# Two-layer graph attention on one core: the shared slot tile is gathered last, and three loads become one transfer each

## The chip, the cores and the metric

The kernel runs on one core of a Trainium2 chip. The metric is the device time of one execution in microseconds (us). The engines are named as the profile names them: PE (matrix products), DVE and ACT (elementwise work), POOL (here it issues the gathers) and SP (here it issues plain transfers). Each engine works through its own instructions in a fixed order and waits on semaphores.

## The reference

A pre-normalised graph network over 3125 nodes with 768 features and 50000 drawn edges plus one self loop per node, sorted by destination (the layer adds a second self loop for every node):

```python
h = jnp.maximum(_layernorm(x, axis=-1), 0.0)
# layer 1: 4 heads x 256, layer 2: 1 head x 768
def gat_conv(x, edge_index, W, a_src, a_dst, bias, heads, out_ch, concat):
    xl = (x @ W).reshape(n, heads, out_ch)
    e = leaky_relu(alpha_src[src] + alpha_dst[dst], 0.2)
    e = exp(e - segment_max(e, dst)[dst])
    alpha = e / (segment_sum(e, dst)[dst] + 1e-16)
    return segment_sum(xl[src] * alpha, dst) + bias
h1 = relu(layer_norm(gat_conv(h, ..., W1, ...), g1, be1)) + (h @ Wr1 + br1)
h2 = layer_norm(gat_conv(h1, ..., W2, ...), g2, be2) + (h1 @ Wr2 + br2)
out = x + h2
```

## The kernel before

Everything is float32. The change touches layer 2 alone. Its nodes are cut into 25 **node tiles** `b` of 128 (the last has 53). The edges of a node tile, sorted by destination, stand in 17 **slot tiles** `j` of 128 slots (`J = 17`; the last node tile has 8). Node tiles hang together in chains of three (`CHAIN = 3`): where `shared(b)` holds, that is for `b` with `b % 3` of 1 or 2, the last slot tile (16) of node tile `b - 1` and the first (0) of `b` are one and the same tile of 128 slots, gathered once. A chain so needs 17 + 16 + 16 = 49 gathers.

For every slot tile POOL issues one indirect transfer (`gather`, lines 206 to 217) that fetches 128 rows of 784 values from the table of layer 2 into one of 36 buffers `g0` to `g35` (`RING = 36`), used in turn. `slots_due` (line 1333) lists the gathers in their planned order, and `fetch` (line 1338) issues them: node tile by node tile, and in a node tile by the five rounds of `ROUNDS = [(0, 5, 9, 13), (1, 6, 10, 14), (4, 11, 15), (2, 8, 16), (3, 7, 12)]`. A gather is issued once the buffer 36 places earlier in the plan is free. Tile 16 stands at the end of round 3, and three tiles of round 4 come behind it. Where it is shared, its buffer is free only after round 0 of the next node tile. The planned order is what the code writes; the order on POOL's own queue is made by a scheduler, which may put a later gather ahead of one whose buffer it expects to come free later. The order on PE, ACT and DVE is written out by hand (`manual_schedule`, line 1465).

The loop over node tiles (line 1482) has the five rounds too. In round `k` of node tile `b`:

- PE adds up the weighted rows of the round's slot tiles (`summed`, line 1421, in a PSUM tile `pa`), which frees their buffers and lets `fetch` go on.
- ACT copies the logits of the gathered rows of node tile `b + 1` into `slots` (`values`, line 1360), at `k` of 0, 1 and 2 for rounds 2, 3 and 4 of that node tile. Rounds 0 and 1 were copied at the end of the node tile before.
- At `k = 2`, once all slot tiles of `b + 1` have landed and are copied, PE transposes them (`mix`, line 1378), and the softmax of `b + 1` follows on DVE and ACT. PE's rounds 3 and 4 of `b` stand behind that transposition in PE's order.
- PE also works at the residual product `pr` (line 1314, recorded as L190) of node tile `b + 3`, eight steps per node tile: one each in rounds 1 and 2, four and then two in round 4.

So PE can't finish node tile `b` before the last gather of node tile `b + 1` has landed.

SP loads, per node tile, `h1` (the residual's input, 512 KB, `load_h1`, in four transfers of two of its eight slices, asked for at residual steps 0 to 3), `xr` (the rows of x, 384 KB, `load_xr`, in two halves, at steps 3 and 4), `own` (the node tile's own rows of the table, 384 KB, `load_own`, in two halves, in rounds 0 and 1) and `hot` (80 KB). In the built program SP's and ACT's transfers use eight semaphores in turn, and POOL's eight others: a transfer waits for the landing of the earlier one that had its semaphore. So at most eight gathers are on their way at once, and SP gets held up where eight of its transfers are.

Of the kernel before, what the change touches and what calls it, by code (L numbers as in the profile page):

```python
# [69 lines left out]
def in_order(  # L70
# [59 lines left out]
    def tiles_of(b):  # L130
        return J if b < NB - 1 else JL
# [1100 lines left out]
    with tc.tile_pool(name="m2", bufs=1, reuse_waits="tile") as mp, \  # L1232
# [35 lines left out]
        for k in range(NK2):  # L1268
            nc.gpsimd.dma_start(wr2[:, k, :], Wr2[k * 128:(k + 1) * 128, :])

        def load_h1(b, q=nc.sync, ks=slice(0, NK2)):
            if b < NB:
                if b not in h1s:
                    h1s[b] = small([128, NK2, P], "h1", bufs=3)
                r = rows_of(b)
                q.dma_start(h1s[b][:, ks, :r], h1T_d[b][:, ks, :r])

        def load_xr(b, cs=slice(0, C2)):
            if b < NB:
                xr = xrs[b] = xrs.get(b) or small([128, C2], "xr", bufs=5)  # L1280
                load_rows(nc.sync, xr[:, cs], x[:, cs], b)

        load_h1(0, nc.gpsimd)
        load_h1(1, nc.gpsimd)
# [17 lines left out]
        def residuals():  # L1302

            for b in range(NB):
                h1, xr = h1s.pop(b), xrs[b]
                r = rows_of(b)
                pm = pp.tile([P, 2, 512], F32, name="pr")
                for k in range(NK2):
                    if k < NK2 // 2:
                        load_h1(b + 2, ks=slice(2 * k, 2 * k + 2))  # L1310
                    if k in (3, 4):
                        load_xr(b + 1, slice((k - 3) * f, (k - 2) * f))
                    for i in range(2):
                        dense(pm[:, i, :f], h1[:, k, :], wr2[:, k, i * f:(i + 1) * f], r,
                              start=(k == 0), stop=(k == NK2 - 1), at=half_at(b, i).start)
                    if k == NK2 - 1 and r == P:
                        nc.vector.tensor_add(pm[:, :, :f], pm[:, :, :f], halves(ball_b))
                        nc.vector.tensor_add(halves(xr), pm[:, :, :f], halves(xr))
                    elif k == NK2 - 1:
                        nc.vector.tensor_add(xr[:r], xr[:r], ball_b[:r])  # L1320
                        for i in range(2):
                            cs = slice(i * f, (i + 1) * f)
                            nc.vector.tensor_add(xr[:r, cs], pm[half_at(b, i), i, :f], xr[:r, cs])
                    yield
# [3 lines left out]
        def filled(n):  # L1328
            for _ in range(n):
                next(fill, None)  # L1330

        gs = {}
        slots_due = [(b, j) for b in range(NB) for k in ROUNDS for j in k
                     if j < tiles_of(b) and not (j == 0 and shared(b))]
        order_of = {s: i for i, s in enumerate(slots_due)}
        asked, unused = 0, set(range(len(slots_due)))

# [9 lines left out]
                    gs[b + 1, 0] = g  # L1347
                asked += 1

        def load_own(b, cs=slice(0, C2)):  # L1350
            if b < NB:
                if b == NB - 1 and b not in owns:
                    owns[b] = small([128, NK2, P], "h1", bufs=3).rearrange("p k n -> p (k n)")[:, :C2]
                own = owns[b] = owns.get(b) or small([128, C2], "own")
                load_rows(nc.sync, own[:, cs], table2[:, cs], b)

        def values(b, k):
            for j in ROUNDS[k]:
# [106 lines left out]
        with tc.manual_schedule(engines={PE, ACT, DVE}):  # L1465
# [16 lines left out]
            for b in range(NB):  # L1482
                pa = pp.tile([P, 2, 512], F32, name="pa", bufs=2)
                opened = set()
                last = b + 1 == NB - 1
                for k in range(len(ROUNDS)):
                    if last and k == 0:
                        load_own(b + 1)
                        for i in range(2, len(ROUNDS)):
                            values(b + 1, i)  # L1490
                        made = softmax(b + 1)
                        next(made)
                    summed(b, k, pa, opened)
                    if k < 2:
                        next(ending, None)
                        if 0 < b < NB - 1:
                            load_own(b, slice(k * f, (k + 1) * f))
                    if b + 1 < NB and not last:
                        if k < 3:
                            values(b + 1, k + 2)  # L1500
                        if k == 2:
                            made = softmax(b + 1)
                            next(made)
                    if k == 2:
                        for _ in ending:
                            pass
                    if k == 4:
                        ending = finish(b, pa)
                        next(ending)
                    if k == 4:  # L1510
                        filled(STEPS[k])
                    if b + 1 < NB and k == (1 if last else 4):
                        next(made)
                        next(made, None)
                        totals2(b + 1)
                        if last:
                            own_share(b + 1)
                    filled(REST if k == 4 else STEPS[k])
                if b + 2 < NB:
                    values(b + 2, 0)  # L1520
                    values(b + 2, 1)
# [474 lines left out]
```

## Time and profile before

| | |
|---|---|
| time, median of 3 runs | 1760.58 us (1757.6 to 1760.94) |
| the profiled execution | 1760.3 us, of which the span from the first to the last instruction is 1758.5 us |
| PE busy | 1632.8 us (93% of the span) |
| DVE, ACT, POOL busy | 1005.1, 457.3, 872.0 us |
| layer 2: first gather issued, last gather issued, end | 1187.73, 1725.4, 1758.5 us |
| gathers of layer 2 | 400, of 401 KB each where all 128 rows are fetched |
| moved by DMA between 1240 and 1690 us | 168.48 MB, 374 GB/s |

A row of a timeline or of a chain begins with the start in us from the span's start and the duration in us; then come engine, line, operation and tiles. In square brackets stands how long the engine was idle before it and what ended that. Gathers are named here by node tile and slot tile, (6,12) for instance, by counting POOL's gathers from the first of the layer and taking their tiles from the built order.

### The profile page before, as it was taken

How to read it: one execution, taken by the hardware profiler on the slowest of the kernel's cores; microseconds unless marked ns; L12 is line 12 of the kernel's file. 1: busy time of each engine (PE TensorE's matmuls, PEld its weight loads, DVE VectorE, ACT ScalarE, POOL GpSimd, SP SyncE). 2: the span in 40 equal slices, each digit the busy share in tenths (PEclk: the TensorE clock that was granted, in tenths of full speed). 3: DMA queues.
4: the chain of work that ended last, by engine and by line, in shares of the span. 5: the costliest groups of instructions: out<-in, count | busy, mean ns of one | idle time of the engine just before them, and what ended most of it. 6: DMA issues, size and time to landing. Idle time of an engine off the chain costs nothing.

```text
span 1758.5 us, 31362 instructions
## 1 busy us (share of the span) xinstructions
PE 1632.8 (93%) x11522; PEld 936.7 (53%) x11522; DVE 1005.1 (57%) x2604; ACT 457.3 (26%) x1312; POOL 872.0 (50%) x908
## 2 busy tenths in 40 slices
PE   7999999999989999999999999997988988988984
PEld 5666666566656556556556555544444443443431
DVE  7784343788864566556565566641444544544545
ACT  2222342000122112212122122122333433433432
POOL 2000012100055766667666667627767667667662
PEclk9999999899989999999999999998999999989987
DMA  7833546533189999999999999969999999999994
GB/s 241 280 120 110 147 129 208 233 132 129 37 313 369 409 400 404 393 403 409 404 393 406 375 374 387 399 228 373 373 370 395 370 359 396 371 357 392 364 328 156
DMA packets 188644, 546.69 MB, mean 311 GB/s; under 512 B 32120, under 2 KB 80632, under 8 KB 188354
## 3 DMA queue, kind: packets, MB, share of 16 engines
q0 software_dynamic: 99632, 386.94, 57.9%
q1 hardware_dynamic: 84456, 147.27, 23.9%
q10 hardware_dynamic: 4394, 10.39, 1.5%
q8 instruction: 94, 1.54, 0.4%
q14 instruction: 68, 0.56, 0.1%
HBM read 492.19 MB, written 65.62 MB: 317 GB/s over the span
## 4 chain that ended last, share of the span: by engine, by line
PE 76%; DMA 14%; DVE 5%; issue 2%; ACT 2%; POOL 1%; SPq 0%; POOLq 0%; DVEq 0%; ACTq 0%
PE pr L190 18%; PE p L190 13%; PE pm L190 12%; PE pa L775 11%; PE pm L1027 7%; PE pa L1421 6%; DMA g<-table,idx_s 5%; DMA g<-table,hi_s 4%; PE pq L580 3%; PE mix L1378 1%; DMA w<-in_L_gnn_W_dram 1%; PE p L1190 1%; DMA h<-h1T_d 1%; DMA s<-slo_d 1%; PE pt L859 1%
## 5 line engine op out<-in xcount | busy, mean ns | idle before, releaser
L210 POOL DMA_INDIRECT g<-table,idx_s x393 | 378.8, 964 | 358.4 <-PE pq L610 170.9
L214 POOL DMA_INDIRECT g<-table,hi_s x423 | 433.6, 1025 | 203.8 <-issue 85.3
L190 PE MATMUL pr<-wr,h 128*128 128x384 f32 x768 | 277.3, 507 | 2.9 <-issue 2.1
L190 PE MATMUL p<-w,h1T 128*128 128x384 f32 (+1 forms) x768 | 267.7, 496 | 0.0
L775 PE MATMUL pa<-g,w 128*32 128x256 f32 x3912 | 246.7, 386 | 8.3 <-DVE w L752 5.6
L190 PEld LDWEIGHTS pr<-wr,h 128*128 128x128 f32 x768 | 143.7, 197 | 112.8 <-issue 35.9
L190 PEld LDWEIGHTS p<-w,h1T 128*128 128x128 f32 x768 | 139.8, 189 | 113.0 <-issue 21.4
L775 PEld LDWEIGHTS pa<-g,w 128*32 128x32 f32 x3912 | 119.7, 110 | 128.3 <-issue 23.8
L1421 PE MATMUL pa<-g,w 128*32 128x384 f32 x1956 | 176.7, 499 | 2.6 <-DVE v L1455 2.6
L752 DVE TENSOR_TENSOR w<-oh,al 128x128 f32<-128x128 f32 (+1 forms) x416 | 132.3, 318 | 51.9 <-PE pa L775 27.2
L190 PE MATMUL pr<-h0k,wr 128*128 128x256 f32 (+1 forms) x576 | 143.0, 395 | 2.5 <-DMA h0k<-h0T_d 2.5
L1027 PE MATMUL pm<-h0g,wr 128*128 128x512 f32 x288 | 133.1, 609 | 0.0
L190 PE MATMUL pm<-w,h0g 128*128 128x344 f32 x432 | 131.5, 459 | 0.3 <-ACT h0g L861 0.3
L190 PE MATMUL pm<-w,h0l 128*128 128x344 f32 x432 | 129.5, 454 | 0.0
L190 PEld LDWEIGHTS pr<-h0k,wr 128*128 128x128 f32 x576 | 106.9, 192 | 32.7 <-issue 10.7
L958 POOL DMA_DIRECT2D hot_d<-ohd x25 | 13.4, 535 | 213.2 <-DVE own L531 123.6
L1421 PEld LDWEIGHTS pa<-g,w 128*32 128x32 f32 x1956 | 57.5, 111 | 113.1 <-issue 104.7
L751 DVE TENSOR_SCALAR oh<-iota_f,rel_s 128x32 f32<-128x32 f32 (+1 forms) x416 | 114.4, 275 | 3.7 <-issue 3.5
L190 PEld LDWEIGHTS pm<-w,h0g 128*128 128x128 f32 x432 | 81.6, 193 | 40.1 <-issue 1.4
L190 PEld LDWEIGHTS pm<-w,h0l 128*128 128x128 f32 x432 | 80.5, 190 | 39.1 <-issue 0.2
L1382 DVE CUSTOM_DVE_ANT_0 mix<-mix,pen 128x640 f32<-128x640 f32 x25 | 20.8, 832 | 129.7 <-PE mix L1378 129.7
L1223 DVE COPY asad<-p 128x2 f32<-128x2 f32 (+1 forms) x25 | 4.0, 159 | 155.3 <-ACT row L1221 155.3
(295 smaller groups left out, 1751.4 us busy)
## 6 DMA issues: line engine op xcount, KB each, us to landing
s<-slo_d SPq DMA_DIRECT2D x25, 544.0 KB
table<-row SPq DMA_DIRECT2D x24, 512.0 KB
own<-table SPq DMA_DIRECT2D x24, 512.0 KB
h1T_d<-h1T SPq DMA_DIRECT2D x24, 512.0 KB
h<-h1T_d SPq DMA_DIRECT2D x88, 128.0 KB
table<-row SPq DMA_DIRECT2D x24, 392.0 KB
ring<-in_x_dram SPq DMA_DIRECT2D x24, 384.0 KB
out_dram<-z ACTq DMA_DIRECT2D x24, 384.0 KB
```

The source lines that it names most:

```text
L190: nc.tensor.matmul(out_, lhsT, rhs, start=start, stop=stop)
L210: nc.gpsimd.indirect_dma_start(out=g, out_offset=None, in_=table[:, :], in_offset=bass.IndirectOffsetOnAxis(ap=idx_s[:, c], axis=0))
L214: nc.gpsimd.indirect_dma_start(out=g, out_offset=None, in_=table[:, :], in_offset=bass.IndirectOffsetOnAxis(ap=idx_k[:, c], axis=0), bound ...
L580: nc.tensor.matmul(q[:, j], oh[:P, o:o + 128], tabs[:, i], start=(i == 0), stop=(i == 2))
L751: nc.vector.tensor_scalar(oh, iota_f[:, lo:hi], rel_s[:, c:c + 1], None, op0=OP.is_equal)
L752: nc.vector.tensor_tensor(w, oh[:, None, :].to_broadcast([128, heads, hi - lo]), al[:, POS[j], :, b:b + 1].to_broadcast([128, heads, hi - ...
L775: nc.tensor.matmul(pa[p0:p0 + 32, o // f, o % f:o % f + n], w[:, o // cols, :], g[:, o:o + n], start=to not in opened, stop=False, skip_gr ...
L859: nc.tensor.transpose(pt[:, k, :r], xt[:, (k0 + k) * 128:(k0 + k + 1) * 128], ident[:r, :r])
L1027: nc.tensor.matmul(pm, wr1[:, k, m * 128:(m + 1) * 128], groups[gi][:, k, :], start=(k == 0), stop=(k == NK1 - 1))
L1190: nc.tensor.transpose(pt[:, k, :r], z[:, (k0 + k) * 128:(k0 + k + 1) * 128], ident[:r, :r])
L1382: nc.vector.tensor_tensor_reduce(out=sums_, in0=sums_, in1=pen, scale=1.0, scalar=-BIG, op0=OP.add, op1=OP.max, accum_out=top)
L1421: nc.tensor.matmul(pa[p0:p0 + 32, i, :f], w_, g[:, i * f:(i + 1) * f], start=(i, q) not in opened, stop=False, skip_group_check=True)
```

## The change

The gathers of a node tile that shares its last slot tile with the next one are reordered in the plan: slot tile 16 comes after 3, 7 and 12 in place of before them (`due`). When its values are copied and when it is summed is as before. Besides, `h1`, `xr` and `own` are loaded by one transfer each: `h1` at residual step 1, `xr` at step 3, `own` in round 0. The bytes are the same.

```diff
-        def load_h1(b, q=nc.sync, ks=slice(0, NK2)):
+        def load_h1(b, q=nc.sync):
             if b < NB:
-                if b not in h1s:
-                    h1s[b] = small([128, NK2, P], "h1", bufs=3)
+                h1s[b] = small([128, NK2, P], "h1", bufs=3)
                 r = rows_of(b)
-                q.dma_start(h1s[b][:, ks, :r], h1T_d[b][:, ks, :r])
-
-        def load_xr(b, cs=slice(0, C2)):
+                q.dma_start(h1s[b][:, :, :r], h1T_d[b][:, :, :r])
+
+        def load_xr(b):
             if b < NB:
                 xr = xrs[b] = xrs.get(b) or small([128, C2], "xr", bufs=5)
-                load_rows(nc.sync, xr[:, cs], x[:, cs], b)
+                load_rows(nc.sync, xr, x, b)
...
                 for k in range(NK2):
-                    if k < NK2 // 2:
-                        load_h1(b + 2, ks=slice(2 * k, 2 * k + 2))
-                    if k in (3, 4):
-                        load_xr(b + 1, slice((k - 3) * f, (k - 2) * f))
+                    if k == 1:
+                        load_h1(b + 2)
+                    if k == 3:
+                        load_xr(b + 1)
...
-        slots_due = [(b, j) for b in range(NB) for k in ROUNDS for j in k
-                     if j < tiles_of(b) and not (j == 0 and shared(b))]
+
+        def due(b):
+
+            js = [j for k in ROUNDS for j in k if j < tiles_of(b) and not (j == 0 and shared(b))]
+            return sorted(js, key=lambda j: j == J - 1) if shared(b + 1) else js
+
+        slots_due = [(b, j) for b in range(NB) for j in due(b)]
...
-        def load_own(b, cs=slice(0, C2)):
+        def load_own(b):
             if b < NB:
                 if b == NB - 1 and b not in owns:
                     owns[b] = small([128, NK2, P], "h1", bufs=3).rearrange("p k n -> p (k n)")[:, :C2]
                 own = owns[b] = owns.get(b) or small([128, C2], "own")
-                load_rows(nc.sync, own[:, cs], table2[:, cs], b)
+                load_rows(nc.sync, own, table2[:, :C2], b)
...
                     if k < 2:
                         next(ending, None)
-                        if 0 < b < NB - 1:
-                            load_own(b, slice(k * f, (k + 1) * f))
+                        if k == 0 and 0 < b < NB - 1:
+                            load_own(b)
```

The first place where it shows is **POOL's queue at the end of node tile 3's gathers**. `g29_12765` is buffer 29 for the gather (3,12) before; the rows above it are (3,2), (3,8), then the shared tile (3,16) in `g26_12660`, (3,3) and (3,7), and behind them (4,5), (4,9) and (4,13) in `g30` to `g32`. Before:

```order
L210 DMA g25_12658<-table2_65,idx_s_98 128x784
L214 DMA g26_12660<-table2_65,hi_s_99 128x784
L210 DMA g27_12704<-table2_65,idx_s_98 128x784
L210 DMA g28_12706<-table2_65,idx_s_98 128x784
L210 DMA g30_12767<-table2_65,idx_s_98 128x784
L210 DMA g31_12769<-table2_65,idx_s_98 128x784
L210 DMA g32_12771<-table2_65,idx_s_98 128x784
L210 DMA g29_12765<-table2_65,idx_s_98 128x784
L210 DMA g33_12773<-table2_65,idx_s_98 128x784
```

And now:

```order
L210 DMA g25_12639<-table2_65,idx_s_98 128x784
L210 DMA g26_12641<-table2_65,idx_s_98 128x784
L210 DMA g27_12684<-table2_65,idx_s_98 128x784
L210 DMA g28_12686<-table2_65,idx_s_98 128x784
L214 DMA g29_12696<-table2_65,hi_s_99 128x784
L210 DMA g30_12700<-table2_65,idx_s_98 128x784
L210 DMA g31_12702<-table2_65,idx_s_98 128x784
L210 DMA g32_12750<-table2_65,idx_s_98 128x784
L210 DMA g33_12752<-table2_65,idx_s_98 128x784
```

Before, the scheduler had put three gathers of node tile 4 ahead of node tile 3's last one, whose buffer 29 held the shared tile (1,16); now node tile 3's five last gathers stand together and the shared tile (3,16) is the last of them. The same swap of three places is there for (6,12), (9,12) and so on to (21,12), seven times in all; the first gathers of these node tiles (3,0) and so on also stood behind three others, and now don't.

The second place is **ACT's copies of node tile 3's logits** for rounds 3 and 4. Before:

```order
L1360 ACTIVATE slots1_12190<-g25_12658 128x32
L1360 ACTIVATE slots1_12190<-g26_12660 128x32
L1360 ACTIVATE slots1_12190<-g27_12704 128x32
L1360 ACTIVATE slots1_12190<-g28_12706 128x32
L1360 ACTIVATE slots1_12190<-g29_12765 128x32
```

And now:

```order
L1364 ACTIVATE slots1_12190<-g25_12639 128x32
L1364 ACTIVATE slots1_12190<-g29_12696 128x32
L1364 ACTIVATE slots1_12190<-g26_12641 128x32
L1364 ACTIVATE slots1_12190<-g27_12684 128x32
L1364 ACTIVATE slots1_12190<-g28_12686 128x32
```

ACT's order of slot tiles is the same ((3,8), (3,16), (3,3), (3,7), (3,12)), so the copy of the gather that is issued last now stands ahead of three others.

The third place is **SP's queue at the start of layer 2**. `own` is node tile 0's, the `xr` are node tiles 1 to 4, and the `h` are the residual's inputs from node tile 2 on. Before:

```order
L227 DMA own<-table_65 128x768
L227 DMA xr<-in_x_dram 128x384 x4
L1258 DMA hot<-hot_d 128x640
L227 DMA xr<-in_x_dram 128x384 x2
L1276 DMA h_12306<-h1T_d 128x256 x4
L227 DMA xr<-in_x_dram 128x384 x2
L1276 DMA h_12333<-h1T_d 128x256 x4
L1276 DMA h_12397<-h1T_d 128x256 x4
L1258 DMA hot<-hot_d 128x640
```

And now:

```order
L227 DMA own<-table_65 128x768
L227 DMA xr<-in_x_dram 128x768 x2
L1258 DMA hot<-hot_d 128x640
L227 DMA xr<-in_x_dram 128x768
L1275 DMA h_12308<-h1T_d 128x1024
L227 DMA xr<-in_x_dram 128x768
L1275 DMA h_12331<-h1T_d 128x1024
L1275 DMA h_12391<-h1T_d 128x1024
L1258 DMA hot<-hot_d 128x640
```

The loads keep their places among each other, here and in every later node tile, where SP's sequence is `h1`, `xr`, `own`, `hot` before and now. There are nine transfers to a node tile before and four now, so the eight semaphores go round less often. PE's, ACT's and DVE's instructions keep their order.

## The prediction

> **What bounds the kernel now.** The first view is PE's list of waits over the whole run (what waited for what: us in total, times, longest):
>
> ```profile
> PE mix L1378 <- ACT slots L1360: 72.7, 14, 9.7
> PE pt L859 <- DVE ring L839: 8.7, 2, 7.5
> ```
>
> PE is 93% busy; of what it waits, nearly all is one place in layer 2, the transposition of the copied logits. The second view is PE's timeline there:
>
> ```profile
> 1285.61 1.33 PE L1378 MATMUL mix<-ident,slots 128*128 128x128 f32 x5 [7.13 <-ACT slots L1360]
> ...
> 1300.21 2.79 PE L1421 MATMUL pa<-g,w 128*32 128x384 f32 x32
> ...
> 1305.85 0.77 PE L1378 MATMUL mix<-ident,slots 128*128 128x128 f32 x5
> ...
> 1350.51 1.33 PE L1378 MATMUL mix<-ident,slots 128*128 128x128 f32 x5 [6.95 <-ACT slots L1360]
> ...
> 1365.09 2.79 PE L1421 MATMUL pa<-g,w 128*32 128x384 f32 x32
> ...
> 1523.25 0.77 PE L1378 MATMUL mix<-ident,slots 128*128 128x128 f32 x5 [0.96 <-ACT slots L1360]
> ...
> 1681.89 1.33 PE L1378 MATMUL mix<-ident,slots 128*128 128x128 f32 x5 [7.56 <-ACT slots L1360]
> ```
>
> A long wait comes once per chain of three node tiles, seven times from 1285.61 (for node tile 3) to 1681.89 (for 21); in between PE waits about 1 us or not at all (1305.85, 1523.25). What ends it is on ACT's timeline, which is the third view, for the wait at 1350.51:
>
> ```profile
> 1336.29 1.16 ACT L1360 ACTIVATE slots<-g 128x32 f32<-128x32 f32 x9
> ...
> 1345.44 0.23 ACT L1360 ACTIVATE slots<-g 128x32 f32<-128x32 f32 x1 [0.81 <-DMA g<-table,idx_s]
> 1350.23 0.23 ACT L1360 ACTIVATE slots<-g 128x32 f32<-128x32 f32 x1 [4.56 <-DMA g<-table,idx_s]
> ```
>
> The last copies are those of (6,7) and (6,12). Gathers before them landed about 1.2 us apart, but between these two there are 4.8 us. The fourth view, POOL's timeline, says why:
>
> ```profile
> 1302.44 0.94 POOL L210 DMA_INDIRECT g<-table,idx_s  x1 [3.71 <-PE pa L1421]
> ...
> 1337.70 0.95 POOL L210 DMA_INDIRECT g<-table,idx_s  x1 [0.30 <-ACT slots L1360]
> 1338.95 0.96 POOL L210 DMA_INDIRECT g<-table,idx_s  x1 [0.30 <-issue]
> 1340.22 0.95 POOL L210 DMA_INDIRECT g<-table,idx_s  x1 [0.30 <-issue]
> 1341.47 0.95 POOL L210 DMA_INDIRECT g<-table,idx_s  x1 [0.30 <-issue]
> 1342.72 0.95 POOL L210 DMA_INDIRECT g<-table,idx_s  x1 [0.30 <-ACT slots L1360]
> ...
> 1362.83 0.96 POOL L210 DMA_INDIRECT g<-table,idx_s  x1 [0.30 <-issue]
> 1367.32 0.94 POOL L210 DMA_INDIRECT g<-table,idx_s  x1 [3.53 <-PE pa L1421]
> ...
> 1700.18 0.94 POOL L210 DMA_INDIRECT g<-table,idx_s  x1 [3.94 <-PE pa L1421]
> ```
>
> (6,7) is issued at 1337.70, then (7,5), (7,9), (7,13), and (6,12) only at 1342.72. POOL issues one gather per 1.254 us (0.95 and a gap of 0.30) whatever happens, except where the ring is full: at 1302.44, 1367.32 and so on it had been idle until PE's round 0 of node tiles 3, 6, ... freed a buffer.
>
> So layer 2 runs in a **loop** of one chain: round 0 of node tile 3 (PE 1300.21) lets POOL go on (1302.44); 32 gathers later (6,12) is issued (40.28 us); it is copied 7.51 us after that; PE goes on 0.28 later (1350.51); PE's rest of node tile 5 and round 0 of node tile 6 take 16.81 up to POOL's next release (1367.32). The sum is 64.88 us; over six loops, from 1302.44 to 1700.18, the mean is 66.29. Two floors lie below it. PE alone needs less (it waits). POOL alone, at 49 gathers of 1.254, needs 61.4. The DMA engines are the third thing near its limit:
>
> ```profile
> 600.00:800.00 200.00, 199.70 (x1665) 117.20 (x1664) 120.13 (x402) 40.49 (x114) 135.10 (x133) 1.00 1.02 401
> 1240.00:1690.00 450.00, 397.53 (x2495) 192.26 (x2488) 208.14 (x386) 178.60 (x546) 320.48 (x336) 0.94 1.01 374
> 1260.00:1300.00 40.00, 32.87 (x191) 16.76 (x189) 16.51 (x32) 15.35 (x46) 29.58 (x31) 0.91 1.02 389
> 1320.00:1360.00 40.00, 33.05 (x218) 15.88 (x211) 18.62 (x34) 14.97 (x42) 30.47 (x32) 0.91 1.03 394
> ```
>
> The last column of these stretches is GB/s: 374 on average in layer 2, 389 and 394 where POOL doesn't pause, 401 in layer 1. The third from last is PE's granted clock.
>
> **The order of the gathers.** The built order puts (6,16) where (7,5) was, at 1338.95 in place of 1342.72: three gathers earlier, 3.77 us. Its buffer was freed in round 4 of node tile 4, some 20 us before, so it waits for nothing. The landing moves with it. Against that, ACT copies (6,16) ahead of (6,3), (6,7) and (6,12), which have landed: three copies more behind the awaited one, 1.16 us / 9 = 0.13 each, 0.39 together. PE goes on 3.77 - 0.39 = 3.38 us earlier, at each of the seven waits.
>
> Where does it go? PE's round 0 releases POOL 3.38 earlier; POOL was idle there 3.5 to 3.9, of which 0.30 is its usual gap, so it takes up all of it. The loop becomes 66.29 - 3.38 = 62.91, still 1.5 above POOL's floor. After the last loop nothing is moved: node tile 23 doesn't share its last slot tile with 24. Sum: 7 x 3.38 = **23.7 us**. Late next is the same landing: PE still waits some 3.6 to 4.2 us there (6.95 to 7.56 less 3.38). The gathers for the other two node tiles of a chain have little slack (0.96 at 1523.25), and PE now comes 3.4 us earlier for them: waits of a microsecond or so will appear there, but they cost nothing as long as the long one behind them ends with a landing that POOL's count sets.
>
> After a wait of 6.95 the transposition takes 1.33, after one of 0.96 it takes 0.77, so PE's clock has sunk in the long ones (0.91 in both stretches that hold one, 1.00 in layer 1). Whether 3.6 to 4.2 us still sinks it lies between a wait of 2.65 (quoted below at 1235.13, matmuls as fast as ever) and those of 7. I take it as sunk, so nothing is gained there; if not, PE's 16.81 shrink by 1.4 or so (0.56 of the transposition, the rest in the matmuls behind it), and POOL's floor decides. The Trainium skill (TensorE: Matmul & The Clock Gate, Part 1) has the clock halve after an idle window of about 3.4 us. The rows agree with that from both sides; by it most of these waits would still be cold, which gives my sum, and the first rival's if the waits come out a little shorter.
>
> **The merged loads.** The same bytes in larger pieces; the queues between 1240 and 1690 us (packets, MB, share of 16 engines' time):
>
> ```profile
> q0 software_dynamic: 26922, 133.18, 77.9%
> q1 hardware_dynamic: 26286, 27.37, 18.6%
> q10 hardware_dynamic: 2736, 7.47, 4.2%
> ...
> h<-h1T_d SPq DMA_DIRECT2D x74, 128.0 KB
> own<-table SPq DMA_DIRECT2D x40, 192.0 KB
> xr<-in_x_dram SPq DMA_DIRECT2D x38, 192.0 KB
> ```
>
> q1 holds SP's loads: 27.37 MB in 18.6% of 16 x 450 us, 20.4 GB/s per engine; the results on q10, whose rows are whole, get 24.7, the gathers 23.7. At q10's rate q1's bytes take 231 us of engine time less, 14 us of all 16 engines in 450, or 3% of the DMA time. This lies beside the loop, not on it, and I count 0. It is cover: a loop of 62.91 needs 374 x 66.29 / 62.91 = 394 GB/s, which is what the stretch at 394 moves. Unmerged loads would leave no room, merged ones some 3%. Bounds: at best the landing of 7.51 gets shorter by 0.2 (3% of it), 1.5 us over the seven; at worst the rival below. SP's own issuing is no term: SP waits for data and semaphores, nobody for SP.
>
> **The start of layer 2.** Here the merge changes when loads go out. Two pieces of the chain of waits, then SP's and PE's timelines:
>
> ```profile
> 1188.94 11.96 DMA own<-table
> 1200.92 18.07 DMA h<-h1T_d
> ```
>
> ```profile
> 1193.63 0.33 SPq L1258 DMA_DIRECT2D hot<-hot_d  x1
> ```
>
> ```profile
> 1210.22 2.46 SPq L227 DMA_DIRECT2D xr<-in_x_dram  x2
> 1214.67 17.37 SPq L1276 DMA_DIRECT2D h<-h1T_d  x8
> ```
>
> ```profile
> 1216.96 1.33 PE L1378 MATMUL mix<-ident,slots 128*128 128x128 f32 x5 [9.72 <-ACT slots L1360]
> 1219.12 7.65 PE L190 MATMUL pr<-wr,h 128*128 128x384 f32 x16 [0.83 <-DMA h<-h1T_d]
> ...
> 1235.13 2.79 PE L1421 MATMUL pa<-g,w 128*32 128x384 f32 x32 [2.65 <-DVE v L1455]
> ```
>
> `h1` of node tile 2 waits until `own` has landed (1200.92), as its semaphore comes round; with half the transfers it has the semaphore that `hot` got at 1193.63 before. So it lands before PE wants it, and PE's 0.83 go. But `xr` of node tile 4 and `h1` of 3 and 4 (0.39 + 0.52 + 0.52 = 1.43 MB) can go out too before node tile 0's last gather, which PE waits for at 1216.96. If all of it lands ahead, that is 1.43 MB / 394 GB/s = 3.6 us. Bounds -0.8 and +3.6; I take +1.0, since the last of it waits for PE's second residual block, and all of it shares the engines with the gathers. All that follows moves along.
>
> **Sum** against the profiled run's own 1760.3 (span 1758.5 and 1.8 around it; the median of the runs is 1760.58, 0.3 above): 1760.3 - 23.7 + 1.0 = **1737.6 us**, and about 1738 as a median.
>
> **The rivals.**
>
> *POOL's floor.* If PE's clock holds, the loop falls to 61.4: 1760.3 + 1.0 - 3.4 - 6 x 4.9 = 1728.5. For it: the waits come out near the 2.65 that did no harm. Against it: every loop would have to run without a single pause of POOL's.
>
> *The landing gets longer.* With POOL hardly pausing the DMA engines never drain, and each landing takes 1 to 2 us more: 1738 + 7 x (1 to 2) = 1745 to 1752. For it: 394 needed where 389 to 394 is what was moved in such stretches. Against it: larger pieces.
>
> *The other waits count.* Waits for the other two node tiles of a chain add up with the long one, up to 1.2 each: the gain falls to 1 us a loop, 1754. Against it: the long wait has 3 us to swallow them.
>
> *Slower: the merged loads stand ahead of the awaited gather.* `h1`, `xr` and `own` of a node tile, 1.31 MB, no longer trickle in small pieces between gathers but go in front of them: 1.31 / 394 GB/s = 3.3 us on a landing of 7.5, and the order's gain is spent. Past 10.0 us (eight gathers of 1.254 on their way) POOL itself is held up, as perhaps already once at the start:
>
> ```profile
> 1226.92 0.95 POOL L210 DMA_INDIRECT g<-table,idx_s  x1 [1.66 <-issue]
> ```
>
> A landing of 10.8 would hold it 0.8 us at each load of the chain (three node tiles), 7 x 2.4 = 17 us: 1777. Where only the awaited landing is hit, 1761. Against it: SP issued these pieces back to back before, too (eight in 17.37 us only where semaphores lacked). The Trainium skill (DMA: Bandwidth & Descriptors, Queues, rings and completion order) has each DMA engine go round its queues a packet at a time. By that rule larger packets do give SP's queue a larger share against the gathers; no row here shows it yet.
>
> That the change doesn't do what it says is answered by the built order: the three places are gone.
>
> **How the numbers follow.** Forecast 0.57 (own range 1731 to 1744); POOL's floor 0.14; longer landings 0.13; the other waits 0.08; slower 0.08. 0.2% (3.5 us) is about what a measurement of this kernel tells from no change. Faster: 0.57 + 0.14 + 0.13 and half of the other waits, 0.88; the same: the other half and a quarter of the last case, 0.06; slower: 0.06. The range, 1728 to 1752, takes in the floor, the start's bounds and the longer landings.
>
> **What would show it.** Right: the last copy of node tile 6 is (6,12) with its gather long landed, and the awaited one, (6,16), starts some 1.2 us behind (6,7)'s place; the seven waits at `mix` fall to 3 to 4 us; POOL's idle before its releases all but goes; layer 2 moves about 394 GB/s. Wrong: landings from issue to copy well over 8 us, POOL idle on `issue` over 0.3 in midstream, long waits for the other two node tiles, or round 0 of node tile 0 later than 1239.

## The result, and the profile after

| | before | after |
|---|---|---|
| median, same chip | 1758.0 us (5 runs, 1757.6 to 1760.94) | 1746.25 us (5 runs, 1738.72 to 1747.39) |
| ratio, 95% interval | | 0.9916 [0.9893, 0.9940] |
| profiled execution | 1760.3 us, span 1758.5 | 1742.3 us, span 1740.5 |
| DMA packets, of them under 2 KB | 188644, 80632 | 172393, 55625 |

The change gains 0.84% (0.6 to 1.07%): 11.75 us between the medians, 18.0 between the two profiled executions. The executions of the changed kernel scatter more (8.7 us against 3.3), and the profiled one is among its shorter ones. What follows is read from it.

PE's list of waits (us in total, times, longest):

```profile
PE mix L1382 <- ACT slots L1364: 53.4, 16, 11.9
```

19.3 us less than before, though the count went from 14 to 16 and the longest, at the start of the layer, from 9.7 to 11.9. PE's timeline shows which became shorter and which are new:

```profile
1285.04 0.98 PE L1382 MATMUL mix<-ident,slots 128*128 128x128 f32 x5 [3.58 <-ACT slots L1364]
...
1347.19 1.33 PE L1382 MATMUL mix<-ident,slots 128*128 128x128 f32 x5 [3.62 <-ACT slots L1364]
...
1388.20 0.77 PE L1382 MATMUL mix<-ident,slots 128*128 128x128 f32 x5 [1.78 <-ACT slots L1364]
1411.15 0.80 PE L1382 MATMUL mix<-ident,slots 128*128 128x128 f32 x5 [4.06 <-ACT slots L1364]
...
1559.14 1.33 PE L1382 MATMUL mix<-ident,slots 128*128 128x128 f32 x5 [2.71 <-ACT slots L1364]
...
1602.09 0.77 PE L1382 MATMUL mix<-ident,slots 128*128 128x128 f32 x5 [3.87 <-ACT slots L1364]
...
1665.89 1.33 PE L1382 MATMUL mix<-ident,slots 128*128 128x128 f32 x5 [5.49 <-ACT slots L1364]
```

The waits once per chain fell from about 7 us to between 3.6 and 5.5, at node tile 15 even to 0.24, with 2.71 at the next one (1559.14); for the other two node tiles of a chain waits of 1 to 3 us came up (1388.20 as well; the one there was 1.31 before). Their cause is again on ACT's and POOL's timelines, here for node tile 9:

```profile
1402.41 0.23 ACT L1364 ACTIVATE slots<-g 128x32 f32<-128x32 f32 x1 [1.32 <-DMA g<-table,idx_s]
...
1405.94 0.33 ACT L1364 ACTIVATE slots<-g 128x32 f32<-128x32 f32 x2
1410.52 0.58 ACT L1364 ACTIVATE slots<-g 128x32 f32<-128x32 f32 x4 [4.25 <-DMA g<-table,hi_s]
```

```profile
1302.09 0.95 POOL L210 DMA_INDIRECT g<-table,idx_s  x1 [1.76 <-PE pa L1425]
...
1338.49 1.01 POOL L214 DMA_INDIRECT g<-table,hi_s  x1 [0.30 <-issue]
...
1364.12 0.95 POOL L210 DMA_INDIRECT g<-table,idx_s  x1 [0.67 <-PE pa L1425]
...
1401.71 1.01 POOL L214 DMA_INDIRECT g<-table,hi_s  x1 [0.30 <-issue]
...
1683.82 0.95 POOL L210 DMA_INDIRECT g<-table,idx_s  x1 [2.63 <-PE pa L1425]
```

The gather waited for is now the shared tile's (`hi_s`). (9,16) is issued at 1401.71, its copy starts at 1410.52, 8.81 us later, three others behind it in the same x4; PE goes on at 1411.15. POOL's idle before its releases went from 3.5 to 4.0 us to between 0.3 and 2.9. The loop, release to release, is (1683.82 - 1302.09) / 6 = 63.62 us, from 66.29. The landing of a gather is here the time from its issue to the start of its copy on ACT. Averaged over the six loops, in us:

| part of the loop | before | after | difference | predicted |
|---|---|---|---|---|
| release to the issue of the awaited gather | 40.55 | 36.82 | -3.73 | -3.77 |
| issue to the start of its copy (landing) | 7.90 | 8.72 | +0.82 | 0 |
| start of the copy to PE | 0.28 | 0.63 | +0.35 | +0.39 |
| PE to the next release | 17.56 | 17.45 | -0.11 | 0 |
| loop | 66.29 | 63.62 | -2.67 | -3.38 |

Six loops give -16.0. The first release is 0.35 earlier (1302.44 to 1302.09), and from the last release to the end it is 56.6 in place of 58.3 us: together -18.0, the whole difference of the spans. Two stretches by engine (the last three columns are PE's granted clock, DMA share and GB/s):

```profile
1240.00:1690.00 450.00, 416.67 (x2631) 200.02 (x2627) 216.04 (x401) 181.06 (x568) 330.64 (x347) 0.96 1.01 384
...
1320.00:1360.00 40.00, 36.09 (x227) 17.85 (x220) 18.95 (x34) 14.47 (x41) 30.25 (x32) 0.96 1.01 394
```

Layer 2 now moves 384 GB/s, 374 before. At the start of the layer, SP's queue and then PE's:

```profile
1193.04 0.33 SPq L1275 DMA_DIRECT2D h<-h1T_d  x1
...
1197.88 11.07 SPq L1275 DMA_DIRECT2D h<-h1T_d  x2
```

```profile
1220.45 1.33 PE L1382 MATMUL mix<-ident,slots 128*128 128x128 f32 x5 [11.86 <-ACT slots L1364]
...
1236.47 4.22 PE L1425 MATMUL pa<-g,w 128*32 128x384 f32 x32 [2.65 <-DVE v L1459]
```

`h1` of node tile 2 goes out 7.9 us earlier, that of 3 16.8 and that of 4 some 15 earlier; node tile 0's last gather lands later, and its `mix` starts 3.5 us later than before. Round 0 of node tile 0 starts 1.3 us later and, with the granted clock at 0.50 from 1237.67 on, takes 4.22 in place of 2.79.

### The profile page after: what moved, and what is told of

Same layout as the page of the kernel before. It is cut to its first block, busy times and chain, and to the rows that moved or that the text cites. A ratio compares the mean times of both kernels' runs of the same rounds, so it can differ in the third digit from the quotient of the medians.

```text
span 1740.5 us, 31246 instructions
## 1 busy us (share of the span) xinstructions
PE 1635.5 (94%) x11522; PEld 936.5 (54%) x11522; DVE 1006.3 (58%) x2604; ACT 453.8 (26%) x1312; POOL 872.4 (50%) x908
## 2 busy tenths in 40 slices
DMA packets 172393, 546.67 MB, mean 314 GB/s; under 512 B 30259, under 2 KB 55625, under 8 KB 172104
## 4 chain that ended last, share of the span: by engine, by line
PE 72%; DMA 16%; DVE 4%; issue 2%; ACT 2%; POOL 2%; POOLq 0%; SPq 0%; DVEq 0%; ACTq 0%
PE pr L190 16%; PE p L190 13%; PE pm L190 12%; PE pa L775 11%; DMA g<-table,hi_s 8%; PE pm L1027 7%; DMA g<-table,idx_s 6%; PE pa L1425 5%; PE pq L580 3%; POOL g L210 2%; PE mix L1382 1%; DMA w<-in_L_gnn_W_dram 1%; PE p L1190 1%; ACT slots L1364 1%; DMA s<-slo_d 1%
## 5 line engine op out<-in xcount | busy, mean ns | idle before, releaser
L520 ACT ACTIVATE bn_sd<-bn_mv,eps 128x1 f32<-128x1 f32 (+1 forms) x50 | 14.7, 295 | 278.4 <-DVE bn_mv L516 267.1
```

## The experiments

Four theories stood at the outset. A: the gain is the order's alone, the merge only costs at the start, and the landings grow because POOL pauses less. B: the larger pieces are what holds up the awaited gathers. C: the merge brings a gain of its own. D: the DMA engines' throughput sets the pace, whatever the order.

The kernels ran on three chips, and on two of them the kernel before is itself about 9% slower: its median is 1924 us on chip B, 1926 to 1927 on chip C, 1758 on chip D. A chip of the first kind is one like D and like that of the result, called the first chip here. Ratios are always to the kernel before on the same chip.

| kernel | chip | median, us | ratio, 95% interval |
|---|---|---|---|
| order alone | B | 1923.21 | 0.9996 [0.9982, 1.0009] |
| merged loads alone | B | 1909.14 | 0.9928 [0.9909, 0.9947] |
| changed, first loads in pieces | B | 1919.59 | 0.9966 [0.9945, 0.9987] |
| changed, 33 buffers | B | 1881.99 | 0.9758 [0.9737, 0.9779] |
| changed | C | 1904.25 | 0.9869 [0.9841, 0.9898] |
| order alone | C | 1923.48 | 0.9977 [0.9958, 0.9996] |
| changed, first loads in pieces, shared copy last | C | 1923.5 | 0.9977 [0.9954, 1.0000] |
| merged loads at the start alone | C | 1914.29 | 0.9937 [0.9909, 0.9964] |
| changed, 30 buffers | C | 1889.47 | 0.9786 [0.9724, 0.9848] |
| changed, without loads of h1 and own | C | 1912.23 | one run |
| changed, with a part of pa left out | C | 1917.51 | one run |
| changed, POOL rests | D | 1771.18 | 1.0081 [1.0060, 1.0102] |

### The parts by themselves (chip B)

Order alone: the kernel before with the new plan of gathers, loads in pieces.

```diff
-        slots_due = [(b, j) for b in range(NB) for k in ROUNDS for j in k
-                     if j < tiles_of(b) and not (j == 0 and shared(b))]
...
+        slots_due = [(b, j) for b in range(NB) for j in due(b)]
```

> The kernel before with the new gather order alone; all loads in pieces as before. Theory A (the gain is the order's, the start's loss is the merge's, and the awaited gathers land later because POOL pauses less, not because pieces are larger): the start of layer 2 is as before (round 0 of node tile 0 at about 1235), the loop is 63 to 64 us in place of 66.3, issue to copy of the awaited gather 8.5 us or more, time 1758 - 21 = 1737 us. Rival B (the larger pieces make the awaited gathers land later): issue to copy stays at 7.9, the loop is 62.9, time 1734 us or less.

Merged loads alone: the changed kernel with the old plan.

```diff
...
-        slots_due = [(b, j) for b in range(NB) for j in due(b)]
+        slots_due = [(b, j) for b in range(NB) for k in ROUNDS for j in k
+                     if j < tiles_of(b) and not (j == 0 and shared(b))]
```

> The change with the old gather order: only the merged loads. Theory A: round 0 of node tile 0 about 1.3 us and of node tile 1 about 3 us late, issue to copy of the awaited gather as before (7.9 us), loop 66.3, time 1758 + 3 = 1761 us. Rival B: issue to copy 8.7 us, loop 67.1, time 1758 + 3 + 6 = 1767 us. Rival C (the merge relieves the DMA engines and is worth something by itself): loop 65 or less, time 1755 us or less.

First loads in pieces: the changed kernel, with `h1` and `xr` of the node tiles up to 5 as before the change.

```diff
...
-                    if k == 1:
+                    if b + 2 <= START and k < NK2 // 2:
+                        load_h1(b + 2, ks=slice(2 * k, 2 * k + 2))
+                    if b + 2 > START and k == 1:
                         load_h1(b + 2)
...
```

> The change, but h1 and xr of node tiles up to 5 still go in pieces, as before; from node tile 6 on they are merged. Theory A: the start is as before again (round 0 of node tile 0 at about 1235, of node tile 1 at 1254), the loops as in the change: 3 us less than the change, 1743 us. If the late start has another cause than the earlier loads, nothing changes: 1746 us.

33 buffers:

```diff
-        RING = 36
+        RING = 33
```

> The change with a ring of 33 gather buffers in place of 36. Theory A (a loop through the ring sets the pace): each buffer less is one gather of 1.254 us more in the loop, three are 3.76, of which about 0.8 comes back as the landings get shorter again: 7 x 3 = 21 us more than the change, 1767 us, with POOL idle 4 us again before its releases. Rival D (DMA throughput alone sets the pace): the same as the change within 3 us, 1746 us.

What was measured turned the expectations round: order alone is worth nothing here, the merged loads 0.7%, the changed kernel with its first loads in pieces 0.3%, and with a ring of 33 buffers it takes 2.4% less than the kernel before. The four expectations were for a kernel before of 1758 us and can't be judged here, theory D and the ring of 33 included. So chip B had to be read before anything could be said about the change.

### The changed kernel, order alone and a mended start (chip C)

> The changed kernel itself, beside its parts. Theory A (the gain is a PE wait on the mixes that gets shorter): where the kernel before takes about 1758 us and PE waits 50 us or more on its mixes, the ratio is 0.990 to 0.994 (1740 to 1748 us), the seven mixes of the order waiting 3.5 to 5.5 us each; where PE loses over 5 us in every node tile to pauses that no landing explains, and so waits on no mix, only the merged loads are left, and the ratio is that of the merged loads alone, 0.991 to 0.995. Rival: the two parts add up wherever the kernel runs, and the ratio is 0.992 in both cases.

> Order alone, loads in their old pieces, once more, beside the changed kernel. Theory A, where the kernel before takes about 1758 us: the seven waits fall from 6.5 to 7.7 us to 3.5 to 4.5 as in the changed kernel, the start is not late (node tile 1's first round at 1254 us, not 1257), so 3 us under the changed kernel: 1737 to 1743, ratio 0.988 to 0.991; issue to copy of the awaited gathers stays 8.5 to 9.2 us, because the landings are longer from POOL's shorter pauses. Rival B (it is the larger pieces that make the landings longer): issue to copy back at 7.9 us, the waits under 3.2, 1732 to 1737. Rival C (the merged loads bring a share of the gain): 1747 to 1752. Where PE waits on no mix before the change, order alone is worth nothing, ratio 0.998 to 1.001.

The third kernel has the first loads in pieces, as above, and ACT copies the shared tile behind the other three:

```diff
-            for j in ROUNDS[k]:
+            js = ROUNDS[k]
+            if shared(b + 1):
+                js = {3: (2, 8), 4: (3, 7, 12, J - 1)}.get(k, js)
+            for j in js:
```

> The changed kernel with the loads of the first node tiles in pieces again and with the copy of the shared tile made last on ACT. Theory A, where the kernel before takes about 1758 us: the start comes back by 2 to 3 us and each of the seven mixes starts 0.3 us after its copy's start instead of 0.6, so 5 us under the changed kernel: ratio to the kernel before 0.987 to 0.990. Rival: both are covered by the next wait, and it takes as long as the changed kernel within 2 us. Where PE waits on no mix: as the changed kernel, within 0.3%.

Chip C behaves like B. PE's waits between 1290 and 1830 us in order alone, and the row of that stretch by engine:

```profile
PE pr L190 <- issue: 49.8, 51, 2.3
PE pa L1426 <- issue: 24.3, 48, 1.6
```

```profile
1290.00:1830.00 540.00, 450.06 (x2409) 203.30 (x2411) 204.38 (x376) 167.71 (x532) 307.67 (x323) 0.89 0.89 301
```

In 540 us there is not one wait at `mix<-ident,slots`. PE pauses instead in its own stream, on nothing that the profile shows, and a node tile takes 27.5 us (the mean from the `mix` of node tile 3 to that of 21), against 22.0 before and 21.2 after on the first chip. With such pauses every awaited gather lands in time. With the old order the wait is all but absent here as well: in the kernel with merged loads at the start alone (below), chip C, the same stretch has

```profile
PE mix L1383 <- ACT slots L1365: 4.2, 4, 1.2
```

while on the first chip the seven long waits before the change come to 50 us. That is the test that theory A asked for: where PE waits on no mix, moving the awaited gather forward is worth 0.0% (B) and 0.2% (C).

The third kernel, 0.9977, lost all that the merged loads bring; whether the copy's place matters can't be seen where no `mix` waits.

The merged loads act at the start. PE's second residual block and VectorE's addition that takes it over, in order alone on chip C:

```profile
1225.39 12.25 PE L190 MATMUL pr<-wr,h 128*128 128x384 f32 x32 [2.10 <-issue]
1245.44 1.33 PE L1383 MATMUL mix<-ident,slots 128*128 128x128 f32 x5 [7.80 <-issue]
```

```profile
1264.94 0.97 DVE L1317 TENSOR_TENSOR pr<-pr,ball_b 128x768 f32<-128x768 f32 x1 [39.65 <-remote]
```

By these rows PE is done at 1237.64 and at its next work at 1245.44, and DVE, idle for 39.65 us, begins only at 1264.94. In the changed kernel on the same chip:

```profile
1246.50 0.97 DVE L1316 TENSOR_TENSOR pr<-pr,ball_b 128x768 f32<-128x768 f32 x1 [20.79 <-remote]
```

18.4 us sooner. The `mix` of node tile 1 follows at 1271.84 in place of 1288.36, 16.5 us, most of the 19.2 us between the medians of the two kernels. On the first chip DVE took this block at 1207.28 before, right after PE.

### What chip C waits for

Four kernels. Merged loads at the start alone, old order:

```diff
-                    if k < NK2 // 2:
+                    if b + 2 <= START and k == 1:
+                        load_h1(b + 2)
+                    if b + 2 > START and k < NK2 // 2:
                         load_h1(b + 2, ks=slice(2 * k, 2 * k + 2))
...
```

> The kernel before with h1 and x by one DMA each for the first node tiles alone (up to node tile 5), everything after in pieces, the old order. Theory S (where the kernel before takes about 1925 us, the merged loads gain at the start of layer 2 alone, where the second residual's sums are handed from PE to VectorE late): mix of node tile 1 about 14 to 17 us earlier, ratio 0.990 to 0.994, the same as all loads merged. Rival M (every merged load saves a share): 6 of 25 node tiles, ratio 0.997 to 0.999. Where the kernel before takes about 1758 us both expect a loss of 2 to 3 us from the start, ratio 1.001 to 1.002.

0.9937: theory S, not the share by node tiles of rival M. The `mix` of node tile 1 came at 1277.06, 11 us earlier than in order alone, a little less than expected.

30 buffers (`RING = 30`):

> The changed kernel with 30 gather buffers instead of 36. Where the kernel before takes about 1925 us: 33 buffers gave 0.976; if what helps is that fewer transfers are under way, 30 goes further (0.965 to 0.975); if 33 only met another phase of PE's pauses, 30 is anywhere from 0.975 to 0.990 and its pauses are as long as with 36 (PE's pauses without a releaser over 80 us). Where the kernel before takes about 1758 us: POOL is released three to six gathers later in each node tile, its stalls grow to over 4 us each and the time rises to 1765 to 1800.

0.9786, neither of the two as they were stated. Between 1290 and 1830 us the pauses all but go, and waits on the landings stand in their place:

```profile
PE mix L1382 <- ACT slots L1364: 95.5, 20, 6.6
PE mix L1382 <- issue: 6.3, 1, 6.3
PE pr L190 <- issue: 1.5, 2, 0.8
```

A node tile takes 25.8 us (26.4 with 33 buffers, in an execution 17 us above that kernel's median). Fewer buffers trade the one wait for the other. Which of the two sizes is better isn't known: they ran on different chips, and their intervals overlap.

Without the loads of `h1` from node tile 3 on and of `own` from 1 to 23:

```diff
-            if b < NB:
-                h1s[b] = small([128, NK2, P], "h1", bufs=3)
+            if 3 <= b < NB:
+                h1s[b] = h1_kept[b % 2]
+            elif b < NB:
+                h1s[b] = h1_kept[b % 2] = small([128, NK2, P], "h1", bufs=3)
...
-            if b < NB:
+            if 0 < b < NB - 1:
+                owns[b] = own_kept
+            elif b < NB:
```

> The changed kernel without the loads of h1 from node tile 3 on and of own rows from node tile 1 to 23 (the old tiles are read again, so the sums are of other rows): 0.9 of some 9.6 MB per node tile less to move, every instruction of PE, VectorE and ScalarE as before. Theory D (where the kernel before takes about 1925 us, PE's pauses come from the transfers beside them): pauses shorter by a tenth or more in proportion to the bytes, period of a node tile from 27.3 to under 25.5 us, 1850 to 1880 us. Theory Q (they come from PE's own dense runs of short matmuls): period within 0.7 us of 27.3, 1885 to 1910 us.

With 24 of 80 matmuls of `pa` left out:

```diff
-            order = [(i, m) for i in range(2) for m in made]
+            order = [(i, m) for i in range(1 if k and b < NB - 1 else 2) for m in made]
```

> The changed kernel with the matmuls of pa for the second half of the columns left out in every round but the first (24 of 80 per node tile; these columns then hold round 0 alone), the transfers as before: 2.1 us less of PE per node tile at full clock. Theory Q (PE's pauses come from its own dense runs of short matmuls): the pauses shrink by more than half, from 8 to under 4 us a node tile, period 27.3 to under 22, 1740 to 1790 us. Theory D (they come from the transfers beside them): the pauses stay, only the 2.1 us are gained, period 25 to 25.5, 1845 to 1870 us.

The same stretch, first without the loads, then with less of `pa`:

```profile
1290.00:1830.00 540.00, 454.10 (x2439) 208.17 (x2440) 206.49 (x380) 171.27 (x544) 312.11 (x328) 0.88 0.81 271
```

```profile
1290.00:1830.00 540.00, 363.86 (x1757) 165.23 (x1756) 199.82 (x371) 165.50 (x533) 305.76 (x322) 0.81 0.85 300
```

The changed kernel on this chip moves 302 GB/s in that stretch, has PE busy for 452.51 us and takes 27.4 us per node tile, so about 8.3 MB (the expectation's 9.6 is too high). Without 0.9 MB of these a node tile takes 27.0 us, without 89 us of PE's work 27.5. Neither kernel gains what theory D or theory Q asked of it, so neither the transfers' volume nor PE's work alone paces this chip; each rests on one run. The second kernel shows the same lateness as the start. PE's transposition back of the softmax, and DVE's copy of it:

```profile
1508.15 0.71 PE L1398 MATMUL mix<-ident,e 128*128 128x128 f32 x5
```

```profile
1520.26 0.69 DVE L1401 COPY w<-mix 128x512 f32<-128x512 f32 x1 [4.73 <-remote]
```

On PE's timeline this is done at 1508.86; DVE, which was late for the work before it as well, starts on it 11.4 us later, after an idle of 4.73. In the profile of the changed kernel on the first chip the same pair is 0.03 us apart:

```profile
1422.76 0.71 PE L1398 MATMUL mix<-ident,e 128*128 128x128 f32 x5
```

```profile
1423.50 0.69 DVE L1401 COPY w<-mix 128x512 f32<-128x512 f32 x1 [4.79 <-PE mix L1398]
```

So on chip C DVE goes on long after PE, by its records, has finished. In order alone on chip B it is the same at the start: PE's second residual block ends at 1233.38, DVE takes it at 1262.71. Whether the message is late or PE's work ends later than the profile says isn't shown.

### Rests on POOL (chip D)

In the starts on B and C the late block reached DVE 48 to 51 us after the layer's first gather in the four kernels where POOL had not paused over 0.6 us, and after 27 to 37 us in the seven where it had paused 0.7 to 1.2 us. Compare the last gather of order alone, and one before the changed kernel's block, both on chip C:

```profile
1260.39 0.95 POOL L210 DMA_INDIRECT g<-table,idx_s  x1 [0.30 <-issue]
```

```profile
1244.02 0.95 POOL L210 DMA_INDIRECT g<-table,idx_s  x1 [1.06 <-DMA g<-table,idx_s]
```

DVE got it 3.6 us after the end of the one's gathers (5.3 to 5.7 in the other three, more than the 2.5 to 4 of the expectation below), and 2.5 us after the other's pause. But the seven are also those whose first loads are merged, so the pause may only go along with it. To test whether POOL's unbroken issuing is the cause:

```diff
...
                 asked += 1
+                if asked % 4 == 0:
+                    nc.gpsimd.memset(rest, 0.0)
```

> The changed kernel with POOL writing 128x600 zeros into a scratch tile after every fourth gather of layer 2: some 0.9 us without a gather issue, about four times per node tile, nothing else changed. Theory R (where the kernel before takes about 1925 us, what PE has finished is seen by the other engines late, because POOL issues gathers without a pause; in the starts so far VectorE saw PE's second residual 2.5 to 4 us after POOL's last gather where there was no pause over 0.6 us, and 10 to 15 us sooner where there was one of about 1 us): the rests let it through, VectorE takes that residual before 1240 us, PE's pauses go from some 8 us a node tile to under 4, and the period falls from 27.3 to POOL's own 16.3 x 1.254 + 4.1 x 0.9 = 24.1, at most 25: 1830 to 1860 us, ratio 0.950 to 0.966, although POOL has more to do. Rival N (POOL's pauses are an effect, and the period is set elsewhere): POOL's stalls shrink by what the rests take, 1895 to 1910 us, ratio 0.985 to 0.992. Rival W (the rests add to the period): 1980 us or more. Where the kernel before takes about 1758 us all three expect a loss, 1795 to 1815 us, since POOL then needs 49 x 1.254 + 12.3 x 0.9 = 72.5 us in a loop of 63.6.

The kernel came to chip D, where the kernel before takes 1758.34 us and nothing is late, so theory R was not tested and stays open. What it shows instead bears on the change. POOL's timeline:

```profile
1407.02 0.95 POOL L210 DMA_INDIRECT g<-table,idx_s  x1 [0.30 <-PE mix L1401]
1407.96 0.62 POOL L1355 MEMSET rest<- 128x600 f32 x1
1408.74 0.95 POOL L210 DMA_INDIRECT g<-table,idx_s  x1 [0.16 <-ACT slots L1367]
```

A rest costs 1408.74 - 1407.02 - 1.254 = 0.47 us, not 0.9, since it takes up part of the usual gap; that is why the loss is 0.8% and not the 2 to 3% expected. POOL then needs 49 x 1.254 + 12.25 x 0.47 = 67.2 us for a loop, and PE's timeline shows the loops:

```profile
1285.03 1.33 PE L1385 MATMUL mix<-ident,slots 128*128 128x128 f32 x5 [4.54 <-ACT slots L1367]
...
1691.40 1.33 PE L1385 MATMUL mix<-ident,slots 128*128 128x128 f32 x5 [6.27 <-ACT slots L1367]
```

(1691.40 - 1285.03) / 6 = 67.7, with no stall of POOL's over 0.6 us between. POOL's count is the bound there, as the prediction had it for its floor: 5.8 us more on POOL's queue cost 4.1 a loop, so less than 2 us of slack were left there. And the landings of the seven awaited gathers take 6.61 to 8.28 us, 7.62 on average, although the loads are merged; over all seven they were 7.87 before and 8.75 after. So the larger pieces by themselves don't lengthen the landing, as theory B had it. Whether they do at the throughput of the change no run shows, since order alone was run on B and C only.

## Why the prediction was right, and where its sizes were off

**The bound and the order of the gathers: right.** The awaited gather is issued 3.73 us earlier in the loop (3.77 predicted) and the three copies cost 0.35 (0.39). That this wait is where the gain comes from is backed from the other side by chips B and C, where PE hardly waits at that place and the order alone gains 0.0 and 0.2%. Order alone on a chip of the first kind was not run, so there the split into parts rests on the table of the loop.

**"The landing moves with it": the step that failed in size.** The likeliest case let the landing stay at its length. It grew by 0.82 us a loop, 1.28 at the first wait, 6.2 us over the seven, and that alone takes the profiled execution from 1737.6 to nearly 1744. The rival for it said 1 to 2 us each and 1745 to 1752. The profiled 1742.3 lies in the likeliest case's own range, while the median of 1746.25 and the two longest executions lie in that rival's. Between the medians the gain is 11.75 us, about half of the 22.7 of the sum; only the profiled execution, the second shortest of its five, is accounted for here. Whether the longer ones have still longer landings isn't known, since only one was profiled in detail. The cause named with the rival, POOL hardly pausing and the DMA engines never draining, is supported, though not separated from the larger pieces at that rate: the sum asked for 394 GB/s, and 389 were moved from 1290 to 1680; with rests for POOL and loads as merged as ever it is 366, and the landings are back at 7.62.

**The merged loads: 0 beside the loop, and nothing in the table of the loop speaks against it.** No run on a chip of the first kind separates them from the order. The slower rival, merged loads ahead of the awaited gather, is out: it asked for landings of 10.8 us, and the longest of the seven is 9.3. By the Trainium skill's rule (DMA: Bandwidth & Descriptors, Queues, rings and completion order), that engines go round their queues a packet at a time, large packets could lengthen the landings; the run with rests has the same packets and the short landings, so there is no sign of it at 366 GB/s.

**The start of layer 2: +1.0 predicted.** Node tile 1's first round came 3.0 us later (1253.95 to 1256.94), but by the issue of (3,16), 2.19 us earlier in place of 3.77, 1.6 us of it were left, within the stated bounds. The step held in kind: `h1` of node tiles 2 to 4 went out early and shared the engines with node tile 0's last gathers. On chips B and C the same step has the other sign, and a size that no bound of the prediction had: -11 to -17 us at the `mix` of node tile 1, against order alone.

**The other waits: no term, right.** They came up as described (1.78, 1.13, 1.98, 2.71) and cost the loop nothing that the table would show; PE's part is 0.11 shorter.

**The clock: taken as sunk, right.** After the wait of 3.62 the transposition takes 1.33. Where it takes 0.77 to 0.98 (after 3.58, 3.87, 4.06) the granted clock falls to 0.50 between 0.4 and 0.8 us after its start; it fell to 0.50 at all seven places but the one with a wait of 0.24. New waits of 2.71 (1559.14) and 1.98 (1516.77) halved the clock as well. The Trainium skill (TensorE: Matmul & The Clock Gate, Part 1) has it halve after an idle window of about 3.4 us that doesn't start with the wait; the seven agree with it, the 2.71 and the 1.98 lie below it. The prediction drew its line between waits of 2.65 and 7, but length alone doesn't decide. The changes of the granted clock lie whole multiples of 3.41 us apart (1237.67, 1285.45 and 1558.52 by 14 and 80 such steps). After the change the wait of 2.65 before round 0 of node tile 0 (1233.82 to 1236.47) has 2.2 us in one step, and the clock falls at that step's end, 1237.67. Before, the equally long wait (1232.48 to 1235.13) was split by a step's end at 1233.91 (three steps after the change at 1223.67), and the clock held.

**POOL's floor: not reached.** The loop is 63.62, 2.2 above 61.4; 0.8 of that is the longer landing, the rest is what the sum had left above the floor.

The tail behind the last release, 1.6 us shorter, had no term. The wait for the landings of node tile 23, which the prediction's list of seven left out, fell there from 7.91 to 5.92; why isn't known. The sum for the profiled execution, against the 22.7 us predicted: 4.7 us less, from the landings (+6.2) and the start (+0.6), less the tail (-1.6) and PE's parts of the loops (-0.5).

## What to carry to other kernels

Moving the awaited transfer forward by n issues gains n issue times at each wait, less what the landing grows by when the issuing engine stops pausing: give the landing a term of its own, from the throughput that the faster loop needs. A gain that is the removal of a wait is worth nothing where the wait isn't; before carrying such a change to another chip, look there whether PE waits at that place. Merging transfers changed here above all when the following ones got their semaphore, so count what it lets out early at the start of a stage.

## What the runs showed that was not expected

The same kernel took 1758 us on two occasions and 1924 to 1927 on chips B and C. From 1290 us on the changed kernel moves 302 GB/s on chip C and 389 on the first, though from 1240 to 1260 us it moved 403 on C, so the DMA engines can go as fast there. What differs is the time from PE's end to the start of the engine that waits for it (11.4 us and 27.3 us in the rows above, 0.03 on the first chip). The period follows neither PE's work nor the bytes moved; at the start of the layer, pauses of POOL go with the end of the lateness, but the run made to show cause and effect came to another chip. Nor is it known whether the recording, under which every run here was timed, takes part in it.

Rings of 33 buffers (0.976, chip B) and 30 (0.979, C) gave the shortest times measured there; the changed kernel with 36 has 0.987 on C, where its interval and that of 30 just overlap. On a chip of the first kind they were not run. That the changed kernel on C (0.987) gains about 0.5% more than the sum of order alone and merged start (0.998 and 0.994) is not explained.
